# Sums of the second softmax one step later, part of their arithmetic on GpSimd and ScalarE

## Chip, cores and metric

The kernel runs on one core of a Trainium2 chip. The metric is device time of the launch in microseconds, median over runs. An engine here is TensorE (PE in the profile; PEld is its weight load), VectorE (DVE), ScalarE (ACT), GpSimd (POOL) or SyncE (SP, which issues DMAs only).

## The reference

x is 8 x 512 x 32 x 32 in fp32, that is 8 images of 512 channels and 1024 positions. Two attention layers follow each other, each with a residual. Layer 0 is a group norm and a plain attention of 8 heads. The change lies in layer 1:

```python
q, k, v = (einsum('oc,bct->bot', w, gn(x)).reshape(b, 8, 64, t) for w in (w_q, w_k, w_v))
attn = einsum('bhdq,bhdT->bhqT', q, k) * scale        # 8 heads, 1024 x 1024
attn = einsum('gh,bhqT->bgqT', w_head, attn)          # heads are mixed before the softmax
attn = softmax(attn, axis=-1)
mean, var = attn.mean((-2, -1)), attn.var((-2, -1))   # of each image and head
attn = (attn - mean) / sqrt(var + eps) * in_gamma + in_beta
out = einsum('bhqT,bhdT->bhqd', attn, v)              # then a projection and the residual
```

The variance needs, for each row of the softmax, the sum of exp and the sum of exp squared: z and z2 below.

## The kernel before, in words

Layer 1 takes the images one by one (class `Attention1`). The 1024 query positions of an image are cut into NT = 8 blocks. A loop runs rounds p = 0 to 8, each with four steps t = 0 to 3 (`step`). A round is a pipeline of three blocks: it computes the scores of block p, mixes and exponentiates block p-1, and multiplies block p-2 with the values. The whole program is in an order written by hand: each engine executes its instructions in the order of the calls in the source. Between engines, waits follow from the tiles that they share.

The calls within a round, with their engines and the lines of the profile:

- `scores(p, i)`, i = 0 to 7: PE multiplies into a PSUM tile of tag "m" (L1628); ScalarE copies it into `raw` (L1640). In round 0 every second copy is DVE's (L1638).
- `regroup`: SP's DMAs bring `raw` into another layout, `re`.
- `mix(p-1, s)`, s = t: PE mixes the heads (L1665) into two tiles of tag "m"; ScalarE writes the exponentials into `e` (L1678), two instructions. Its matmuls alternate between the two tiles.
- `flip(p-1, s)`: DVE transposes `e` into `et` (L1693). `moments(p-1, s)`: four BN_STATS on DVE give count, mean and squared deviations of `e` (L1704).
- `values(p-2, u, parts)`: PE multiplies `et` with v (L1720) into a PSUM tile of tag "a"; `leave(p-2, u)`: ScalarE copies it out (L1736), two instructions.
- `sums(p-2)`: three instructions on DVE (L1746, L1749, L1750) turn the moments into `zz`, the operand for the sums over partitions.
- `totals(p-2)`: two matmuls (four records in the profile, L1757) with `zz` as weights give z and z2, side by side in one PSUM tile of tag "a". Then `reciprocals`: DVE computes rz = 1/z (L1769); POOL issues two DMAs, rz to DRAM (`zd`, L1772) and back, broadcast, into `rzb` (L1779); DVE keeps z in `zs` (L1782), squares rz (L1784), multiplies by z2 and adds up in `s2` (L1786 to L1789).
- `divide`: in even rounds from 4 on, GpSimd multiplies finished values by `rzb` (L1811).

PSUM has three tiles of tag "m" and two of tag "a"; an allocation waits until the readers of the tile that stood in its place are done. An `Agenda` (`ag.run(slot)`) puts work of the next image at given places: products of v (`v_pair`, L1454; one half is copied out by ScalarE, L1458, the other by DVE, L1459), loads, normalization, and in round 8 the next image's k projection (`k_go`, `k_leave`, and `right_y`, additions on DVE).

After round 8 come `sums` and `totals` of the last block, `instance` (DVE sums `s2` into `isb`) and `instance_end` (the matmul `pi`, L1825, and the image's variance).

Of the kernel before, what the change touches and what calls it, by code (L numbers as in the profile page):

```python
# [9 lines left out]
F32 = mybir.dt.float32  # L10
# [8 lines left out]
P = 128  # L19
# [448 lines left out]
def tile_two_attention_layers(  # L468
# [19 lines left out]
    nc = tc.nc  # L488
# [208 lines left out]
    with ExitStack() as l0:  # L697
# [5 lines left out]
        stat = l0.enter_context(tc.tile_pool(name="stat", bufs=2))  # L703
# [368 lines left out]
        def attention0(b, agenda):  # L1072
# [96 lines left out]
            for i in range(0, NI + 2, 2):  # L1169
                if i < NI:  # L1170
                    scores(i)
                    scores(i + 1)
                if i >= 2:
                    for w in (i - 2, i - 1):
                        values(w)
                        sums(w)
                    if (i - 1) % NG == NG - 1:
                        g = (i - 1) // NG
                        agenda.at(i + 2, lambda g=g: totals(g))
                        agenda.at(i + 6, lambda g=g: reciprocals(g))  # L1180
                        agenda.at(i + 10, lambda g=g: finish(g))
                agenda.run(i)
                agenda.run(i + 1)
# [83 lines left out]
    with ExitStack() as l1:  # L1267
# [6 lines left out]
        stat = l1.enter_context(tc.tile_pool(name="stat1", bufs=2))  # L1274
# [166 lines left out]
        def k_leave():  # L1441
            for fn in due:
                fn()
            due.clear()
# [168 lines left out]
        class Attention1:  # L1613
# [127 lines left out]
            def sums(self, p):  # L1741

                bn = self.bn.pop(p).rearrange("p s a (r k) -> p r (s a) k", k=3)
                zz = stat.tile([P, 3, 2, 16], F32, tag="zz", name=f"zz_{self.b}_{p}")
                mean, m2 = bn[..., 1], bn[..., 2]
                nc.vector.tensor_scalar_mul(  # L1746
                    zz[:, 0::2], mean.unsqueeze(1).to_broadcast([P, 2, 2, 16]), float(2 * P)
                )
                nc.vector.tensor_mul(zz[:, 1], mean, zz[:, 0])  # L1749
                nc.vector.tensor_add(zz[:, 1], zz[:, 1], m2)  # L1750
                self.zz = zz

            def totals(self, p):
# [10 lines left out]
            def reciprocals(self, p, ps):  # L1764

                b = self.b
                z, z2 = ps[:32, 0:32], ps[:32, 32:64]
                rz = stat.tile([32, 32], F32, tag="rz", name=f"rz1_{b}_{p}")
                nc.vector.reciprocal(rz, z)  # L1769
                zd = dram.tile([H, P], F32, tag=f"zd_{b}_{p}", name=f"zd_{b}_{p}")  # L1770
                queue = nc.sync if p == NT - 1 else nc.gpsimd
                queue.dma_start(  # L1772
                    out=zd.rearrange("g (x q) -> x g q", q=4),
                    in_=rz.rearrange("x (g q) -> x g q", q=4),
                )
                if p % 2 == 0:
                    self.rzb = zpool.tile([P, T], F32, tag="rzb", name=f"rzb_{b}_{p}")
                h = p % 2 * D
                queue.dma_start(  # L1779
                    out=self.rzb[h : h + D], in_=zd.rearrange("g i -> (g i)").partition_broadcast(D)  # L1780
                )
                nc.vector.tensor_copy(self.zs[:, p], z)  # L1782
                r2 = stat.tile([32, 32], F32, tag="r2", name=f"r2_{b}_{p}")
                nc.vector.tensor_mul(r2, rz, rz)  # L1784
                if p == 0:
                    nc.vector.tensor_mul(self.s2, r2, z2)  # L1786
                else:
                    nc.vector.tensor_mul(r2, r2, z2)
                    nc.vector.tensor_add(self.s2, self.s2, r2)  # L1789

            def check(self):

# [54 lines left out]
            def step(self, p, t, ag):  # L1847

                new, old, older = p < NT, p >= 1, p >= 2
                if t == 0:  # L1850
                    if new:
                        for i in range(3):
                            self.scores(p, i)
                    if older:
                        self.values(p - 2, 0, 2, 3)
                        self.leave(p - 2, 0)
                        self.sums(p - 2)
                        if p % 2 == 0 and p >= 4:
                            self.divide(p // 2 - 2, nc.gpsimd)
                    if old:  # L1860
                        self.mix(p - 1, 0)
                    ag.run(4 * p - 0.5)
                elif t == 1:
                    if older:
                        self.values(p - 2, 1, 0)
                        self.flip(p - 1, 0)
                        self.totals(p - 2)
                        self.moments(p - 1, 0)
                    if new:
                        self.scores(p, 3)  # L1870
                    if old:
                        self.mix(p - 1, 1)
                    ag.run(4 * p + 0.5)
                elif t == 2:
                    if older:
                        self.values(p - 2, 1, 1)
                    if new:
                        self.scores(p, 4)
                        self.scores(p, 5)
                    if old and not new:  # L1880
                        self.mix(p - 1, 2)
                    ag.run(4 * p + 1.5)
                    if older:
                        self.values(p - 2, 1, 2, 3)
                        self.leave(p - 2, 1)
                    if old and new:
                        self.mix(p - 1, 2)
                else:
                    if new:
                        self.scores(p, 6)  # L1890
                        if old:
                            self.values(p - 1, 0, 0)
                        self.scores(p, 7)
                        if old:
                            self.mix(p - 1, 3)
                            self.values(p - 1, 0, 1)
                    else:
                        self.mix(p - 1, 3)
                        self.values(p - 1, 0, 0, 1)
                    ag.run(4 * p + 2.5)  # L1900
                k_leave()
                if p == 1 or old and t:
                    self.flip(p - 1, t)
                    self.moments(p - 1, t)
                if new:
                    for kh, s in (
                        (), ((0, 0), (0, 1), (0, 2)), ((0, 3),), ((1, 0), (1, 1), (1, 2), (1, 3)),
                    )[t]:
                        self.regroup(p, kh, s)
                if old and t == 0:  # L1910
                    self.piece()
                ag.run(4 * p + t)
# [156 lines left out]
```

## Time and profile before

| | us |
|---|---|
| median of 3 runs | 4002.35 (4001.08 to 4011.55) |
| profiled execution, its own time | 3999.31 |
| span of its profile | 3997.5 |
| PE busy in the span | 3885.5 |
| DVE, ACT, POOL busy | 2834.6, 1971.3, 128.5 |
| layer 1, with the end | from about 1830 on |

The span is the time from the first to the last instruction of the profiled execution. A row of a group gives line, engine, operation, tiles and shapes, then busy time and mean duration (ns), then the engine's idle time just before these instructions and what ended it ("<-"). A row of waits gives who waited for whom, the total in us, how often, and the longest. A line of the order of time gives start, duration, engine, line, operation and tiles, and in brackets the idle time before it. A window line gives its length, each engine's busy time with its number of instructions, the granted clock of TensorE, the busy share of the DMA engines and their rate in GB/s.

### The profile page before, as it was taken

The page shows a single profiled execution, that of the slowest core. Times are in us where ns is not written, and L with a number is a line of the kernel's source. Part 1 is how long each engine was busy: PE and PEld are TensorE (multiplying, and loading weights), DVE is VectorE, ACT ScalarE, POOL GpSimd, SP SyncE. Part 2 cuts the span into 40 slices and gives each one's busy share as a digit, 9 for nine tenths or more (in the row PEclk, how much of TensorE's full clock was granted, in tenths as well). Part 3 has the DMA queues.
Part 4 walks back from the last instruction along what each step waited for, and adds up shares of the span by engine and source line. Part 5 has one row for each costly group of instructions (what it writes and reads, how often), then busy time and mean ns, then how long its engine had stood idle before and what let it go on. Part 6 is the DMA issues. An engine that isn't in the chain of part 4 may idle for free.

```text
span 3997.5 us, 95841 instructions
## 1 busy us (share of the span) xinstructions
PE 3885.5 (97%) x41932; PEld 1826.1 (46%) x41932; DVE 2834.6 (71%) x4124; ACT 1971.3 (49%) x2431; POOL 128.5 (3%) x150
## 2 busy tenths in 40 slices
PE   8999999999999999999999999999999999999997
PEld 4353535344343535344544535545545445445354
DVE  4748475766657584857958949859769679588597
ACT  1726363544536271615717528437257166175274
POOL 0000000000000000000100000000001000000010
PEclk9999999999999999999999999999999999999999
DMA  3313131111121111217828749658469288397384
GB/s 121 120 48 117 46 120 48 62 59 66 53 83 54 72 68 61 75 66 184 230 92 226 190 120 237 173 137 227 148 164 228 99 210 207 97 232 198 107 219 127
DMA packets 245883, 519.10 MB, mean 130 GB/s; under 512 B 47312, under 2 KB 54480, under 8 KB 238800
## 3 DMA queue, kind: packets, MB, share of 16 engines
q1 hardware_dynamic: 238912, 497.95, 43.2%
q0 software_dynamic: 6544, 14.94, 1.7%
q8 instruction: 331, 5.42, 0.6%
q14 instruction: 96, 0.79, 0.1%
HBM read 197.16 MB, written 46.92 MB: 61 GB/s over the span
## 4 chain that ended last, share of the span: by engine, by line
PE 81%; DVE 13%; ACT 2%; DMA 2%; issue 2%; SPq 0%; DVEq 0%
PE s L1084 11%; PE a L1110 11%; PE a L1720 7%; PE s L1628 7%; DVE bn L1704 6%; PE pk_p L902 6%; PE pq_p L902 5%; PE pv L1454 5%; PE pv_p L902 5%; DVE et L1693 5%; PE pp_p L902 5%; PE pk L1379 4%; PE pq L1379 4%; PE pp L1379 4%; PE m L1665 4%
## 5 line engine op out<-in xcount | busy, mean ns | idle before, releaser
L1693 DVE STREAM_TRANSPOSE et<-e 128x2048 f32<-128x2048 f32 x256 | 587.3, 2294 | 88.7 <-ACT e L1678 86.8
L1720 PEld LDWEIGHTS a<-et,v 128*64 128x64 f32 x16384 | 509.2, 138 | 296.2 <-issue 247.6
L1704 DVE BATCH_NORM_STATS2 bn<-e 128x6 f32<-128x512 f32 x1024 | 634.3, 675 | 0.0
L1089 ACT ACTIVATE e<-s 128x1024 f32<-128x1024 f32 x512 | 497.2, 1026 | 234.5 <-PE s L1084 232.1
L1640 ACT COPY raw<-s 128x1024 f32<-128x1024 f32 x480 | 470.2, 1018 | 226.1 <-PE s L1628 197.5
L1720 PE MATMUL a<-et,v 128*64 128x64 f32 x16384 | 557.0, 225 | 12.1 <-DVE et L1693 11.4
L1678 ACT ACTIVATE e<-m 128x1024 f32<-128x1024 f32 x512 | 496.2, 1021 | 126.5 <-PE m L1665 54.2
L1097 DVE TENSOR_TENSOR zacc<-zacc,e 128x1024 f32<-128x1024 f32 x384 | 468.7, 1221 | 87.2 <-ACT e L1089 64.9
L1628 PE MATMUL s<-k,q 64*64 64x512 f32 x4096 | 516.0, 608 | 6.2 <-DVE q L1493 3.1
L1084 PE MATMUL s<-q,k 64*64 64x512 f32 x4096 | 490.1, 593 | 2.3 <-ACT e L1089 2.3
L1110 PE MATMUL a<-e,v 64*64 64x512 f32 x4096 | 484.1, 589 | 0.0
L1665 PE MATMUL m<-re,wmix 32*32 32x512 f32 x8192 | 315.3, 604 | 19.3 <-DMA re<-raw 17.8
L1110 PEld LDWEIGHTS a<-e,v 64*64 64x64 f32 x4096 | 156.7, 133 | 282.8 <-issue 282.2
L1084 PEld LDWEIGHTS s<-q,k 64*64 64x64 f32 x4096 | 147.9, 133 | 275.2 <-issue 240.7
L1628 PEld LDWEIGHTS s<-k,q 64*64 64x64 f32 x4096 | 127.7, 132 | 220.8 <-issue 78.2
L1454 PE MATMUL pv<-wv,y 128*128 128x512 f32 x480 | 212.1, 597 | 0.0
L1736 ACT COPY q<-a 64x256 f32<-64x256 f32 x256 | 93.7, 366 | 184.7 <-PE a L1720 182.7
L1772 POOL DMA_DIRECT2D zd<-rz x56 | 34.7, 619 | 3449.0 <-DVE r L1784 3449.0
L1454 PEld LDWEIGHTS pv<-wv,y 128*128 128x128 f32 x480 | 89.3, 190 | 116.9 <-issue 110.3
L1665 PEld LDWEIGHTS m<-re,wmix 32*32 32x32 f32 x8192 | 66.7, 103 | 148.9 <-ACT raw L1640 58.6
L1458 ACT COPY v<-pv 128x512 f32<-128x512 f32 x30 | 17.6, 585 | 218.7 <-PE pv L1454 218.7
L1095 DVE TENSOR_TENSOR zacc<-e,e 128x1024 f32<-128x1024 f32 x64 | 78.3, 1223 | 56.1 <-ACT e L1089 56.1
(315 smaller groups left out, 3942.4 us busy)
## 6 DMA issues: line engine op xcount, KB each, us to landing
re<-raw SPq DMA_DIRECT2D x1024, 256.0 KB
left_q<-left_q SPq DMA_DIRECT2D x17, 1792.0 KB
left_p<-left_p SPq DMA_DIRECT2D x17, 1792.0 KB
left_k<-left_k SPq DMA_DIRECT2D x10, 1792.0 KB
x<-in_x_dram SPq DMA_DIRECT2D x32, 512.0 KB
rzb<-zd SPq DMA_DIRECT2D x128, 128.0 KB
x<-x SPq DMA_DIRECT2D x64, 256.0 KB
y<-x SPq DMA_DIRECT2D x32, 512.0 KB
```

The costliest lines, as they stand in the source:

```text
L902: nc.tensor.matmul(out, st, mv, start=start, stop=(k == 1), skip_group_check=True)
L1084: nc.tensor.matmul(ps[c * D : c * D + D, m], k[r, hp, k0 : k0 + D], q[r, hp, ts(f, FB)], start=True, stop=True,)
L1089: nc.scalar.activation(e[i], ps, AF.Exp, scale=S0 * S0)
L1110: nc.tensor.matmul(acc[g][a][m * D : m * D + D], v[rows, kc, ts(2 * hp + m, D)], e[i][rows, m], start=(kc == 0), stop=(kc == NG - 1),)
L1379: nc.tensor.matmul(self.ps[m][:, i], w[:, left, k * HC + i * P : k * HC + i * P + P], right[:, k], start=(k == 0 and m != 2), stop=(k == 1 ...
L1454: nc.tensor.matmul(ps[:, m], y_t[b][:, c, ts(2 * i + m, P)], w[:, c], start=(c == 0), stop=(c == NCC - 1),)
L1628: nc.tensor.matmul(ps[c * D : c * D + D, m], qo_t[b][r, p, hp, ts(c, D)], k_t[b][r, hp, ts(kh, FB)], start=True, stop=True,)
L1665: nc.tensor.matmul(ps[a // 2][c * 32 : c * 32 + 32, a % 2].rearrange("p (r h k) -> p h r k", r=2, h=2), wmix[rows].rearrange("p g i -> p ( ...
L1678: nc.scalar.activation(e[:, :, 2 * h : 2 * h + 2].rearrange("p r a k -> p a r k"), ps[h].rearrange("p a (r k) -> p a r k", r=2), AF.Exp,)
L1693: nc.vector.transpose(self.et[p, u].rearrange("p kb (r st a) g q -> p st kb r (a g q)", r=2, st=2)[:, st], self.e[p, s].rearrange("p r a ( ...
L1704: nc.vector.bn_stats(self.bn[p][:, s, a], e[:, :, a].rearrange("p r k -> p k r"))
L1720: nc.tensor.matmul(acc[two * D : two * D + D, s].rearrange("p (x q) -> p x q", q=4), v_t[b][:, kb, ts(g, D)], et[:, kb, :, g], start=(kb = ...
```

## The change

It moves `totals(p-2)` from step 1 of a round to step 2, behind one more piece of `values`. It gives the three instructions of `sums` to GpSimd, with one buffer for `zz` instead of two. In `reciprocals` the copy of z goes from DVE to ScalarE, a new ScalarE copy brings z2 to SBUF (`zq`), and the square, product and addition go to GpSimd, which reads `zq` in place of PSUM. DVE keeps the reciprocal. In round 1 the first flip and its moments are called in step 1 and not at the end of step 0.

```diff
@@ sums
-                zz = stat.tile([P, 3, 2, 16], F32, tag="zz", name=f"zz_{self.b}_{p}")
+                zz = stat.tile([P, 3, 2, 16], F32, tag="zz", name=f"zz_{self.b}_{p}", bufs=1)
                 mean, m2 = bn[..., 1], bn[..., 2]
-                nc.vector.tensor_scalar_mul(
+                nc.gpsimd.tensor_scalar_mul(
                     zz[:, 0::2], mean.unsqueeze(1).to_broadcast([P, 2, 2, 16]), float(2 * P)
                 )
-                nc.vector.tensor_mul(zz[:, 1], mean, zz[:, 0])
-                nc.vector.tensor_add(zz[:, 1], zz[:, 1], m2)
+                nc.gpsimd.tensor_mul(zz[:, 1], mean, zz[:, 0])
+                nc.gpsimd.tensor_add(zz[:, 1], zz[:, 1], m2)
@@ reciprocals
-                nc.vector.tensor_copy(self.zs[:, p], z)
+                nc.scalar.copy(self.zs[:, p], z)
+                zq = stat.tile([32, 32], F32, tag="zq", name=f"zq_{b}_{p}")
+                nc.scalar.copy(zq, z2)
                 r2 = stat.tile([32, 32], F32, tag="r2", name=f"r2_{b}_{p}")
-                nc.vector.tensor_mul(r2, rz, rz)
+                nc.gpsimd.tensor_mul(r2, rz, rz)
                 if p == 0:
-                    nc.vector.tensor_mul(self.s2, r2, z2)
+                    nc.gpsimd.tensor_mul(self.s2, r2, zq)
                 else:
-                    nc.vector.tensor_mul(r2, r2, z2)
-                    nc.vector.tensor_add(self.s2, self.s2, r2)
+                    nc.gpsimd.tensor_mul(r2, r2, zq)
+                    nc.gpsimd.tensor_add(self.s2, self.s2, r2)
@@ step, t == 1
                     if older:
                         self.values(p - 2, 1, 0)
+                    if old:
                         self.flip(p - 1, 0)
-                        self.totals(p - 2)
                         self.moments(p - 1, 0)
@@ step, t == 2
                     if older:
                         self.values(p - 2, 1, 1)
+                        self.totals(p - 2)
@@ step, end of each t
                 k_leave()
-                if p == 1 or old and t:
+                if old and t:
                     self.flip(p - 1, t)
                     self.moments(p - 1, t)
```

## The prediction

> **What bounds the kernel now.** I read the busy line first, then the busy time of one round of layer 1, then the waits of layer 1 (1850 us to the end), then the order of time of one round.
>
> ```profile
> PE 3885.5 (97%) x41932; PEld 1826.1 (46%) x41932; DVE 2834.6 (71%) x4124; ACT 1971.3 (49%) x2431; POOL 128.5 (3%) x150
> ```
> ```profile
> 2149.00:2170.00 21.00, 20.81 (x456) 11.21 (x452) 19.78 (x29) 16.91 (x20) 1.43 (x3) 1.00 0.90 240
> ```
> ```profile
> PE z L1757 <- DVE zz L1750: 29.1, 27, 2.1
> PE m L1665 <- DMA re<-raw: 17.8, 11, 3.3
> PE a L1720 <- DVE et L1693: 10.8, 9, 5.3
> PE z L1757 <- ACT e L1678: 3.6, 18, 0.4
> ```
>
> The first line gives TensorE 97% of the span. The second (columns PE, PEld, DVE, ACT, POOL) is the round p = 3 of image 1: PE is busy 20.81 of 21 us, DVE 19.78, ACT 16.91. So a round is TensorE's, with DVE just behind, and microseconds in which PE stands still are lost for good. The waits say where it stands: 29.1 us before the matmuls of `totals`, for the operand `zz`, and 3.6 more where another semaphore was named but `zz` ended just before; the row of these matmuls has 32.8 us of idle time. That is all that the change can give back there.
>
> [...] The trace shows such an ordering, in the one place where both engines read one PSUM tile (`v_pair`; ScalarE takes the first half, DVE the second):
>
> ```profile
> 2097.28 0.58 ACT L1458 COPY v<-pv 128x512 f32<-128x512 f32 x1 [6.89 <-PE pv L1454]
> ...
> 2097.90 0.69 DVE L1459 COPY v<-pv 128x512 f32<-128x512 f32 x1 [6.44 <-ACT v L1458]
> ...
> 2099.19 1.22 DVE L1638 COPY raw<-s 128x1024 f32<-128x1024 f32 x1 [0.60 <-PE s L1628]
> ...
> 2100.05 1.01 ACT L1640 COPY raw<-s 128x1024 f32<-128x1024 f32 x1 [0.70 <-PE s L1628]
> ```
>
> DVE had been idle for 6.44 us, the matmuls were done, and yet it began only as ScalarE's copy ended. The same two engines, writing one SBUF tile from two PSUM tiles, do overlap (last two lines). So it is the shared PSUM tile that orders them. [...]
>
> **The change part by part.** The key is where `totals` lands. In round 3 of image 1, DVE alone and then ScalarE alone, in order of time:
>
> ```profile
> 2155.54 2.31 DVE L1693 STREAM_TRANSPOSE et<-e 128x2048 f32<-128x2048 f32 x1 [1.05 <-ACT e L1678]
> 2157.78 0.31 DVE L1769 RECIPROCAL rz<-z 32x32 f32<-32x32 f32 x1
> ...
> 2158.65 2.51 DVE L1704 BATCH_NORM_STATS2 bn<-e 128x6 f32<-128x512 f32 x4
> 2161.09 2.28 DVE L1693 STREAM_TRANSPOSE et<-e 128x2048 f32<-128x2048 f32 x1
> ```
> ```profile
> 2153.57 1.94 ACT L1678 ACTIVATE e<-m 128x1024 f32<-128x1024 f32 x2 [0.48 <-ACT q L1736]
> 2156.11 1.01 ACT L1640 COPY raw<-s 128x1024 f32<-128x1024 f32 x1 [0.60 <-PE s L1628]
> 2157.32 1.94 ACT L1678 ACTIVATE e<-m 128x1024 f32<-128x1024 f32 x2 [0.20 <-PE m L1665]
> 2159.30 1.93 ACT L1640 COPY raw<-s 128x1024 f32<-128x1024 f32 x2
> 2162.15 0.74 ACT L1736 COPY q<-a 64x256 f32<-64x256 f32 x2 [0.93 <-PE a L1720]
> ```
>
> The reader is to see that DVE does the reciprocal (L1769) between a flip and its moments, and that ScalarE goes straight from the exponentials of mix 1 (end 2159.26) to the `raw` copies of scores 4 and 5. In the same stretch PE has mix 1 at 2155.97, values, scores 4 and 5, values, and mix 2 at 2162.04.
>
> *Moved to t = 2.* PE's `totals` matmuls now stand behind `values(p-2, 1, 1)`; the reciprocal is queued on DVE behind two whole pairs of flip and moments instead of one flip. The `zz` wait goes: -32.8 us.
>
> *New wait.* The copies `zs` and `zq` read the bank that the reciprocal reads, come after it in the program, and are now ScalarE's; so ScalarE waits for DVE's reciprocal. Queued behind them on ScalarE: the `raw` copies of scores 4 and 5, the leave of the values, the exponentials of mix 2. Who waits: mix 2 on PE, which needs two of the three buffers of tag "m", and one is scores 4's.
>
> Replayed on the round above:
> - DVE can't flip e(p-1, 0) before its exponentials end, at 2155.51. A pair takes 4.61 (2161.09 to the next flip at 2165.70), so two end at 2164.76, and the reciprocal (0.31), which stood at 2157.78, at 2165.07. ScalarE is through with mix 1 at 2158.8.
> - `zs` and `zq`: ACT copies of 256 and 512 columns take 366 and 585 ns, by the slope some 0.17 us for 32: 2165.45. Scores 4's `raw` copy then ends at 2166.46, not 2160.3.
> - PE does values, totals, scores 4 and 5 and half of values and is at mix 2 at 2161.85; it begins at 2166.5: **4.65 us idle**. Its matmuls alternate between both buffers, so the free one does not help.
> - After it `raw` 5, leave (0.74) and the exponentials of mix 2 end at 2170.1 and `raw` 6 at 2171.1; PE is at mix 3 at 2170.7: another 0.45.
> - From there each step of PE, ACT and DVE lies later by the same amount up to the next mix 0, so it comes back each round: 5.1 us.
>
> Rounds 2 to 7 of 8 images: 48 x 5.1 = +245 us. Ends: copies of 0.1 or 0.3 us, a wake-up of 0.1 and the position of DVE's other work give 4.2 to 5.8, or +200 to +280.
>
> *Round 8* has no scores; the reciprocal stands behind two more DVE additions of the next image's `right_y`, at about 1999.8 in image 0 instead of 1990.4. Exponentials 2 end at 2002.15, mix 3 begins then and not at 2000.36: 1.8 us, x8 = +14 (0 to 25).
>
> *Taken from DVE:* per round 219 + 216 + 212 (sums), 116 (`zs`), 179 + 175 + 179 (squares): 1.3 us. PE bounds the round, so beyond the `zz` wait it is worth nothing.
>
> *Put on GpSimd:* six small instructions. [...] The three of the operand are ready some 1 us after moments(p-2, 3), which end near the end of mix 0; `totals` comes 4 us later. Cover: these 4 us, and as much again, since PE waits later anyway. If each took over 1.4 us, the `zz` wait would be back, but inside that stall. The squares stand on POOL's queue behind both DMAs (zd lands 4.1 us after issue) and end over 5 us before the next operand is due. POOL's DMAs and `divide` move with the reciprocal, 7 us later; rzb lands in 6.0, before the next even round. Nothing: 0, at most +10.
>
> *`zz` in one buffer:* the next `sums` wants it a round after the matmuls that read it: 0. *Round 1's flip* one step later: DVE has no instruction between the two places: 0. *Ends of images:* `isb` waits for three GpSimd instructions, about 0.6 us of DVE; PE's `pi` comes at 2023.53, 6 us after the sum was ready: 0, at most +5.
>
> **Sum:** -32.8 + 245 + 14 = +226 on the profiled execution's 3999.31 us (span 3997.5): **4225 us**. The median of the runs is 4002.35, 3 us above that execution; I don't add this.
>
> **The rivals.**
> 1. *No order between the readers.* Then ScalarE gains two copies of 0.2 us in a round in which it has 4 us free, DVE is relieved, and PE loses the 32.8 us: 3999.3 - 33 = 3966, or up to 3985 if transfers, 0.90 to 0.95 busy in rounds 1 to 4, give some back. This ends faster. It decides if ScalarE is past `zs` and `zq` by 2160.8, since `raw` 4 is then ready when PE reaches mix 2; a reciprocal one pair earlier would do as well. Against it: the `v` pair, ordered 23 of 23 times that DVE was idle, and the order of the calls. 9%.
> 2. *A smaller stall.* DVE's pairs, or what stands between the reciprocal and mix 2, are shorter than in this round, or PE's idle time absorbs later waits: 3.7 us a round gives 3999.3 - 33 + 178 + 14 = 4158. The pair has 4.61 to 4.63 us in each of three looked at. 6%.
> 3. *GpSimd late on top*: its operand behind `divide` (2.36 us) and the rzb waits, late by more than 8 us in even rounds. 24 rounds x 4 us more: about 4320. The operand stands ahead of `divide` in its queue. 4%.
>
> **How the numbers follow.** My case: 81%, 4225 with its own 4175 to 4275. The range takes in rival 2 and ends short of rivals 1 and 3: 4150 to 4280. Differences within 0.3% (12 us), about what a measurement of this kernel can tell from no change, get 1%, same 0.01: faster 0.08 (rival 1 but for the case that transfers take its gain back), slower 0.91.
>
> **What would show it.** Right: a row of ScalarE copies `zs<-z` with some 6 us idle each, ended by DVE's reciprocal, about 300 us in all; PE's row `m<-re,wmix` idle by over 200 us, ended by the `raw` copies; rounds of 25.9 us; no wait at L1757's matmuls; DVE idle more, not less. Wrong: `zs` starting before the reciprocal, or rounds of 21 us. If GpSimd's three instructions take over 1.4 us each, the waits at `zz` will show that.

## The result, and the profile after

| | before | after |
|---|---|---|
| median, 4 runs of each on one chip | 4002.43 us (4001.08 to 4011.55) | 4264.14 us (4256.06 to 4266.12) |
| ratio after / before, 95% interval | | 1.0645 [1.0624, 1.0666] |
| profiled execution, its own time | 3999.31 | 4264.97 |
| span | 3997.5 | 4263.1 |
| mean granted TensorE clock | 0.995 | 0.971 |

The change makes the kernel 6.4% slower; on the profiled executions it costs 265.7 us where the sum in the prediction has 226. From one image of layer 1 to the next, 311.81 us pass (277.96 before). Inside an image, the time from one round's sums over partitions to the next's is 27.31 us in the mean of rounds 2 to 7 (21.48 before): 5.83 us more, and five such intervals make 29.2 of the 33.85 us.

First the page of the kernel after: its span and busy line, then four groups, with busy time, mean duration (ns), the idle time just before them, and what ended it.

```profile
span 4263.1 us, 96029 instructions
...
PE 4013.6 (94%) x41932; PEld 1861.4 (44%) x41932; DVE 2760.7 (65%) x3684; ACT 1984.7 (47%) x2559; POOL 251.1 (6%) x526
...
L1693 DVE STREAM_TRANSPOSE et<-e 128x2048 f32<-128x2048 f32 x256 | 590.0, 2305 | 430.7 <-ACT e L1678 425.8
...
L1665 PE MATMUL m<-re,wmix 32*32 32x512 f32 x8192 | 393.3, 638 | 198.4 <-ACT raw L1640 174.3
...
L1746 POOL TENSOR_SCALAR zz<-bn 128x64 f32<-128x64 f32 x64 | 36.0, 563 | 3287.6 <-DVE bn L1704 2869.4
...
L1782 ACT COPY zs<-z 32x32 f32<-32x32 f32 x64 | 11.2, 174 | 335.5 <-DVE rz L1769 335.3
```

The last line is the new row that the prediction asked for: ScalarE stands still for 335.3 us before 64 tiny copies, and DVE's reciprocal ends all of it. The mixing row, L1665, now has 198.4 us of idle time (19.3 before), 174.3 of it ended by ScalarE's `raw` copies. There is no row of L1757 with a wait any more. DVE, relieved of 440 instructions, is less busy (2760.7 against 2834.6) and idles more. And one thing is not explained by waits: PE executes the same 41932 instructions, yet is busy 128 us longer (4013.6 against 3885.5). That is taken up below.

The waits of layer 1 say the same by pairs (total us, times, longest), here PE's and then ScalarE's:

```profile
PE m L1665 <- ACT raw L1640: 174.3, 49, 3.9
PE m L1665 <- DMA re<-raw: 18.5, 14, 3.0
PE a L1720 <- DVE et L1693: 6.1, 8, 1.7
```
```profile
ACT zs L1782 <- DVE rz L1769: 335.3, 56, 7.2
```

One round in order of time, DVE alone:

```profile
2168.07 2.31 DVE L1693 STREAM_TRANSPOSE et<-e 128x2048 f32<-128x2048 f32 x1 [0.76 <-ACT e L1678]
2170.31 2.47 DVE L1704 BATCH_NORM_STATS2 bn<-e 128x6 f32<-128x512 f32 x4
2172.70 2.29 DVE L1693 STREAM_TRANSPOSE et<-e 128x2048 f32<-128x2048 f32 x1
2174.92 2.45 DVE L1704 BATCH_NORM_STATS2 bn<-e 128x6 f32<-128x512 f32 x4
2177.29 0.33 DVE L1769 RECIPROCAL rz<-z 32x32 f32<-32x32 f32 x1
2182.57 2.31 DVE L1693 STREAM_TRANSPOSE et<-e 128x2048 f32<-128x2048 f32 x1 [4.96 <-ACT e L1678]
```

ScalarE and then PE in the same stretch:

```profile
2169.58 1.94 ACT L1678 ACTIVATE e<-m 128x1024 f32<-128x1024 f32 x2 [0.50 <-PE m L1665]
2177.65 0.17 ACT L1782 COPY zs<-z 32x32 f32<-32x32 f32 x1 [6.13 <-DVE rz L1769]
2177.73 0.17 ACT L1784 COPY zq<-z 32x32 f32<-32x32 f32 x1
2177.97 1.93 ACT L1640 COPY raw<-s 128x1024 f32<-128x1024 f32 x2
```
```profile
2174.56 1.05 PE L1665 MATMUL m<-re,wmix 32*32 32x512 f32 x4
2179.03 1.49 PE L1665 MATMUL m<-re,wmix 32*32 32x512 f32 x28 [3.42 <-ACT raw L1640]
2180.45 1.98 PE L1628 MATMUL s<-k,q 64*64 64x512 f32 x8
2182.37 1.47 PE L1720 MATMUL a<-et,v 128*64 128x64 f32 x32
```

DVE does two pairs of transpose and BN_STATS without a gap; the reciprocal stands behind them and ends at 2177.62. ScalarE, through with the exponentials of mix 1 at 2171.52, waits 6.13 us for it, and only then copies scores 4 and 5 to `raw`. PE has begun mix 2 with the four records that fit the free buffer and stands for 3.42 us. Then DVE in its turn has nothing to transpose for 4.96 us. The stall runs once around the three engines.

### The profile page after: what moved, and what is told of

The parts are those of the page before. It is cut to its first block, busy times and chain, and to the rows that moved or that the text cites. A ratio compares the mean times of both kernels' runs of the same rounds, so it can differ in the third digit from the quotient of the medians.

```text
span 4263.1 us, 96029 instructions
## 1 busy us (share of the span) xinstructions
PE 4013.6 (94%) x41932; PEld 1861.4 (44%) x41932; DVE 2760.7 (65%) x3684; ACT 1984.7 (47%) x2559; POOL 251.1 (6%) x526
## 5 line engine op out<-in xcount | busy, mean ns | idle before, releaser
L1693 DVE STREAM_TRANSPOSE et<-e 128x2048 f32<-128x2048 f32 x256 | 590.0, 2305 | 430.7 <-ACT e L1678 425.8
L1720 PEld LDWEIGHTS a<-et,v 128*64 128x64 f32 x16384 | 532.5, 144 | 327.7 <-issue 310.7
L1720 PE MATMUL a<-et,v 128*64 128x64 f32 x16384 | 580.1, 230 | 6.7 <-DVE et L1693 6.7
L1665 PE MATMUL m<-re,wmix 32*32 32x512 f32 x8192 | 393.3, 638 | 198.4 <-ACT raw L1640 174.3
L1628 PE MATMUL s<-k,q 64*64 64x512 f32 x4096 | 554.7, 648 | 6.2 <-DVE q L1493 3.1
L1665 PEld LDWEIGHTS m<-re,wmix 32*32 32x32 f32 x8192 | 80.1, 105 | 372.4 <-ACT raw L1640 238.7
L1628 PEld LDWEIGHTS s<-k,q 64*64 64x64 f32 x4096 | 131.2, 138 | 239.1 <-issue 88.9
L1746 POOL TENSOR_SCALAR zz<-bn 128x64 f32<-128x64 f32 x64 | 36.0, 563 | 3287.6 <-DVE bn L1704 2869.4
L1782 ACT COPY zs<-z 32x32 f32<-32x32 f32 x64 | 11.2, 174 | 335.5 <-DVE rz L1769 335.3
L1736 ACT COPY q<-a 64x256 f32<-64x256 f32 x256 | 93.8, 367 | 135.7 <-PE a L1720 133.6
```

What stands on the lines that cost most here:

```text
L1628: nc.tensor.matmul(ps[c * D : c * D + D, m], qo_t[b][r, p, hp, ts(c, D)], k_t[b][r, hp, ts(kh, FB)], start=True, stop=True,)
L1665: nc.tensor.matmul(ps[a // 2][c * 32 : c * 32 + 32, a % 2].rearrange("p (r h k) -> p h r k", r=2, h=2), wmix[rows].rearrange("p g i -> p ( ...
L1693: nc.vector.transpose(self.et[p, u].rearrange("p kb (r st a) g q -> p st kb r (a g q)", r=2, st=2)[:, st], self.e[p, s].rearrange("p r a ( ...
L1720: nc.tensor.matmul(acc[two * D : two * D + D, s].rearrange("p (x q) -> p x q", q=4), v_t[b][:, kb, ts(g, D)], et[:, kb, :, g], start=(kb = ...
```

## The experiments

All ratios are to the kernel before, run on the same chip, with 95% intervals.

**1. The order of the calls on ScalarE.** From the kernel after, the two copies are put ahead of the reciprocal, so that DVE waits for ScalarE and not the other way round:

```diff
+                nc.scalar.copy(self.zs[:, p], z)
+                zq = stat.tile([32, 32], F32, tag="zq", name=f"zq_{b}_{p}")
+                nc.scalar.copy(zq, z2)
                 nc.vector.reciprocal(rz, z)
...
-                nc.scalar.copy(self.zs[:, p], z)
-                zq = stat.tile([32, 32], F32, tag="zq", name=f"zq_{b}_{p}")
-                nc.scalar.copy(zq, z2)
```

> The changed kernel with the two ScalarE copies of z and z2 placed ahead of the reciprocal, nothing else. Theory A (ScalarE's queue stands behind DVE's reciprocal because the readers of one PSUM tile take turns in the order of the program): ScalarE then waits for PE only, DVE waits for ScalarE's copies that are long done; the stall before mix 2 goes, and with it the halved clock after it; PE also keeps the 32.8 us of waits at zz that the change saved: 3966 us, up to 3985 if the transfers give some back. Theory B (what costs is the added work on ScalarE and GpSimd, or the later place of totals): all that is still there, so about 4264, at least over 4200. Idle before zs: under 0.5 us each under A, some 6 us under B.

Measured: 4059.86 us, ratio 1.0134 [1.0116, 1.0151], a round of 22.75 us. Three lines in another place give back 204 of the 262 us. ScalarE's wait for the reciprocal is gone: before `zs` it now stands still for 2.3 us in all, and for PE's sums. But it is not a gain: 56 us above the kernel before, some 75 to 95 above what the theory had.

**2. The copies back on DVE**, all else as in the kernel after:

```diff
-                nc.scalar.copy(self.zs[:, p], z)
+                nc.vector.tensor_copy(self.zs[:, p], z)
-                nc.scalar.copy(zq, z2)
+                nc.vector.tensor_copy(zq, z2)
```

> The changed kernel with the copies zs and zq given to DVE, so that all readers of z are on one engine; the place of totals and the GpSimd work stay. Theory A: no engine waits for another's read, 3966 to 3985 us, as close to e1_scalar_first as 0.3%; the 0.23 us that DVE does more per round lie in its slack. Theory B with GpSimd or the place as the cause: 4200 or more. B with ScalarE's added work as the cause: also near 3970, but then e1_scalar_first stays at 4264.

Measured: 4062.7 us, ratio 1.0140 [1.0123, 1.0157], a round of 22.89 us: the same as with ScalarE first, and the same unexplained rest.

**3. ScalarE's copies alone, at the old place.** From the kernel before: `zs` and `zq` by ScalarE behind the reciprocal, DVE keeps the arithmetic (and reads `zq`), `zz` has one buffer, `totals` stays in step 1. The copies in the diff:

```diff
-                nc.vector.tensor_copy(self.zs[:, p], z)
+                nc.scalar.copy(self.zs[:, p], z)
+                zq = stat.tile([32, 32], F32, tag="zq", name=f"zq_{b}_{p}")
+                nc.scalar.copy(zq, z2)
```

> The kernel before with only the two copies on ScalarE (after the reciprocal), squares on DVE from zq, zz in one buffer; totals stays in step 1, where the reciprocal has one flip ahead of it and not two pairs of flip and moments. Theory A: the stall has the length by which the reciprocal lies behind the point where ScalarE is free. Here that is 2.4 us and not 6.3; replayed on round 3 of image 1, PE is held up at scores 4 and 5 by 1.4 us a round, with no halved clock: 48 x 1.4 = 67, less what the waits at zz had taken anyway: 4040 to 4070 us. Theory B (GpSimd or step 2 costs): 4002, unchanged.

Measured: 4066.65 us, ratio 1.0151 [1.0134, 1.0168], a round of 22.56 us, as expected. One wait of PE's and one of ScalarE's:

```profile
PE s L1628 <- ACT raw L1640: 50.8, 40, 1.5
```
```profile
ACT zs L1782 <- DVE rz L1769: 133.6, 56, 2.6
```

At the old place the reciprocal has only a transpose ahead of it on DVE, not two whole pairs, and ScalarE's wait per round is 2.4 us (133.6 / 56) in place of 6.0 (335.3 / 56). PE meets it at the scores, which need the tiles that `raw` empties. So the copies cost 62 us without the move; the move makes the same wait two and a half times as long.

**4. The move alone.** From the kernel before, `totals` in step 2, everything else DVE's as it was:

```diff
                         self.values(p - 2, 1, 0)
                     self.flip(p - 1, 0)
-                        self.totals(p - 2)
...
                         self.values(p - 2, 1, 1)
+                        self.totals(p - 2)
```

> The kernel before with totals moved from step 1 to step 2 and nothing else: all readers of z and all arithmetic stay on DVE. Theory A: the place itself costs nothing and the waits at zz go, 32.8 us: about 3970 us (3965 to 3985). Theory B, that the later place costs through the later reciprocal, rzb and divide: 4200 or more.

Measured: 4077.94 us, ratio 1.0177 [1.0160, 1.0194], a round of 23.10 us. Both theories missed. The waits of PE show why:

```profile
PE a L1720 <- DVE r L1788: 51.4, 38, 3.0
PE m L1665 <- DMA re<-raw: 48.2, 32, 4.3
PE a L1720 <- DVE s L1786: 12.8, 8, 1.6
```

In one round, DVE's last reader of z, and PE around it:

```profile
2178.45 0.17 DVE L1788 TENSOR_TENSOR r<-r,z 32x32 f32<-32x32 f32 x1
```
```profile
2176.38 1.10 PE L1628 MATMUL s<-k,q 64*64 64x512 f32 x8
2178.68 1.15 PE L1720 MATMUL a<-et,v 128*64 128x64 f32 x32 [1.20 <-DVE r L1788]
```

The first values of a new block, `values(p-1, 0, 0)`, need a PSUM tile of tag "a". There are two. With `totals` in step 2, the one handed to them is z's, and they start only when the last instruction that reads z has ended. In the kernel before no such wait is in the list. DVE comes to it late, behind its two pairs; 64.2 us of PE's time go there, and the wait for the regrouped scores (`re<-raw`) grows from 17.8 to 48.2 us besides. With ScalarE first the same wait is there under another name, since DVE's only read of z is then the reciprocal (L1772 in that kernel); in experiment 2 it is 49.7 us:

```profile
PE m L1665 <- DMA re<-raw: 46.7, 31, 4.6
PE a L1720 <- DVE rz L1772: 43.1, 45, 2.6
```

Together these come near the 56 us of experiment 1, as an estimate: 43.1, and 28.9 more for the transfers, and 16.5 more inside the mixing groups (38.5 us beyond 1.15 us a group, 22.0 in the kernel before), less the 32.8 of `zz`.

**5. The operand alone on GpSimd**, the place and everything else as before:

```diff
-                nc.vector.tensor_scalar_mul(
+                nc.gpsimd.tensor_scalar_mul(
...
-                nc.vector.tensor_mul(zz[:, 1], mean, zz[:, 0])
-                nc.vector.tensor_add(zz[:, 1], zz[:, 1], m2)
+                nc.gpsimd.tensor_mul(zz[:, 1], mean, zz[:, 0])
+                nc.gpsimd.tensor_add(zz[:, 1], zz[:, 1], m2)
```

> The kernel before with the three instructions of the sums' operand on GpSimd and nothing else, totals in step 1. GpSimd needs 1.1 to 1.2 us for them where DVE needed 0.72, so zz comes 0.5 us later after the moments, while DVE is free 0.65 us a round earlier. Where PE waits for zz it waits about 0.5 us longer: up to 4020 us; where DVE's backlog caused the wait, part comes back: 4000 at least.

Measured: 4013.18 us, ratio 1.0030 [1.0018, 1.0041], as expected. The wait before `totals` is longer than DVE's was (29.1 and 3.6):

```profile
PE z L1757 <- POOL zz L1750: 46.2, 47, 2.1
```

So GpSimd is the slower engine for these three, by little (1.18 us together in the kernel after, 0.65 on DVE in the kernel before); one step later that is covered, as the next experiment shows: it has no wait for `zz`.

**6. z's tile freed early.** The first experiment once more, and the reciprocal now reads ScalarE's copy, so that DVE does not touch that PSUM tile at all:

```diff
-                nc.vector.reciprocal(rz, z)
+                nc.vector.reciprocal(rz, self.zs[:, p])
```

> As e1_scalar_first, with DVE's reciprocal taken from the SBUF copy zs and not from PSUM, so that ScalarE is the only reader of z and DVE does not touch that PSUM tile. Theory C (found in e1, e2 and e4: the next values take the PSUM tile of z, and wait there for DVE's last read of it, some 1 us a round): the wait of PE at the first values of step 3 goes, the waits at zz stay away, 3966 to 3985 us. Rival D (what e1 lost lies in the transfers, whose waits had grown to 47 us): they stay, 4020 to 4060.

Measured: 4004.51 us, ratio 1.0004 [0.9995, 1.0013], a round of 21.70 us: between what the two theories had. PE's waits:

```profile
PE m L1665 <- DMA re<-raw: 29.1, 22, 3.9
PE a L1720 <- DVE et L1693: 9.3, 8, 4.9
```

The wait for z's tile is gone, as is that for `zz`; yet the time is that of the kernel before, not 33 us less. The transfers' wait is 11 us longer, and more of it lies inside the mixing groups, where the trace has it as stretched groups and not as idle time ahead of them: what these groups take beyond their usual 1.15 us comes to 47.6 us in layer 1, and to 22.0 in the kernel before. The same with operand and squares back on DVE (and round 1's flip where it was):

> As e7_scalar_first_rz_from_sbuf, with the sums' operand and the squares back on DVE: the kernel before with totals in step 2, ScalarE's two copies first, and the reciprocal and squares from SBUF. Theory C says that no wait hangs on GpSimd: within 0.5% of e7, 3970 to 3995 us, the 1.2 us that DVE does more per round being near its slack. If GpSimd's part is what keeps DVE from falling behind, this one shows waits at et or zz again and is slower than e7 by 10 us or more.

Measured: 4008.1 us, ratio 1.0011 [1.0003, 1.0019]: as near to the other as expected, and like it above what the theory had. GpSimd's part is worth 0.1% of the time at most; the two intervals overlap.

**7. Do the transfers take the gain?** Half of the DMAs of `regroup` in blocks 2 to 7 are left out (`mix` then reads old data there), once in the kernel of experiment 6, once, as a control, in the kernel before:

```diff
-                for r in range(2):
+                for r in range(2 if p < 2 else 1):
```

> As e7_scalar_first_rz_from_sbuf, but of the regrouping DMAs of blocks 2 to 7 only the first of each two is issued, so half of these rows stay as an earlier block left them; transfers of a round fall from 16 of 256 KB to 8. Theory G (what e7 did not gain went to the transfers: raw tiles and re slots are waited for): the waits for re<-raw (29 us) and the waits inside the mix groups (some 25 us more than before) go; rounds of 20.8 us; 3945 to 3970 us. Theory H (they are waits of another kind, or latency that traffic does not set): 3990 to 4005.

> The kernel before with the same half of the regrouping DMAs left out in blocks 2 to 7: the control for e9. Waits for re<-raw (17.8 us) go, in part, and the waits at zz (32.8 us) stay: 3980 to 3995 us under theory G. The difference e10 minus e9 is then what the change of e7 is worth when transfers do not limit: about 30 us; under theory H it is about 0.

Measured: 3944.51 us, ratio 0.9856 [0.9831, 0.9881], and 3971.75 us, ratio 0.9925 [0.9899, 0.9950]. The first lies at the lower end of what its theory had, the control some 8 us below what was expected of it. First the waits of the kernel of experiment 6 with fewer DMAs, then those of the kernel before with fewer:

```profile
PE a L1720 <- DVE et L1693: 10.0, 8, 5.5
PE m L1665 <- DMA re<-raw: 6.3, 8, 2.0
```
```profile
PE z L1757 <- DVE zz L1750: 23.8, 25, 2.1
PE a L1720 <- DVE et L1693: 10.7, 9, 5.3
PE z L1757 <- ACT e L1678: 5.5, 24, 1.1
PE m L1665 <- DMA re<-raw: 3.8, 7, 1.3
```

With fewer transfers the two kernels stand 27 us apart, about the 29.3 us that the second still waits for `zz`; with all transfers they stand level. So 27 of the 33 us can be had, and in the full kernel the regrouping DMAs take them back. Of the 25.6 us more inside the mixing groups, 10 stay with fewer DMAs (29.4 us against 19.3); their cause is not shown.

**8. The clock after the stall.** In the kernel after, matmuls were put into the stall of mix 2, to see whether its cost is the idle time alone. Twice they went into `mix`, for s = 2, ahead of its own matmuls, into the first or the (p % 2)-th of its two tiles:

```diff
+                if s == 2 and 1 <= p < NT - 1:
+                    for _ in range(4):
...
+                                nc.tensor.matmul(
+                                    ps[0][c * D : c * D + D, m], qo_t[b][r, p, 0, ts(c, D)],
+                                    k_t[b][r, 0, ts(0, FB)], start=True, stop=True,
+                                )
```

> The changed kernel with four more groups of score products ahead of mix 2 in rounds 2 to 7, written into the tile that mix 2 then overwrites: added work of about 3.8 us, in place of idle time of about 4.3. Theory E (the part of the loss above the replay is TensorE's granted clock, halved for 3.4 us after each stall): the products after the stall run at full rate again, a round takes about 26 us in place of 27.3, and the time falls although work is added: about 4220 us (4205 to 4240). Rival F (the products after the stall are slow for another reason): no gain, 4264 or above.

> As e5_filled_stall, with the added products written in each round into that one of mix 2's two tiles that is free early (in e5 every other round took the one that waits for raw 4, so its products came after the stall; these rounds took 32 us, the others 25.7). Theory E: all rounds take about 25.75 us in place of 27.3, 48 x 1.55 = 74 us less than the changed kernel although work is added: 4190 us (4180 to 4215). Rival F (no clock effect): 4264 or above.

Measured: 4347.36 us, ratio 1.0862 [1.0846, 1.0878], and 4346.39 us, ratio 1.0862 [1.0834, 1.0889]. Both missed. Rounds alternate between 25.7 and some 32 us: in one the added products stand in the stall, in the next they wait for a tile that comes free only after it, and the stall follows on top. The second was to pick the free tile by the block's parity and did not; which tile is free early was not settled. Even so the two say something of the clock: in both, the 24 rounds with the filled stall (25.4 us in the mean) have no period of halved clock, and each of the 24 long ones has one. A third form needs no tile of its own, as scores 5 are computed five times over into their own tile, ahead of the stall:

```diff
-                for c in range(2):
+                for c in [0, 1] * (5 if i == 5 and p >= 2 else 1):
```

> The changed kernel with the products of scores 5 issued five times over into the same tile in rounds 2 to 7 (the last writes the result): 3.7 us of added products in each round, in a tile that is free when PE comes to it in every round, ahead of the values and of mix 2, and so inside the stall. Theory E (the loss above the replay is the clock halved after each stall): no round has a halved clock after mix 2, each takes about 25.8 us in place of 27.3: about 4190 us (4180 to 4215), less than the changed kernel with 180 us of products added. Rival F: 4264 or above.

Measured: 4193.85 us, ratio 1.0489 [1.0469, 1.0508], a round of 25.69 us. PE does more work, and the kernel is 70 us faster than without it (62 by the two ratios). The page's busy line, one round (columns: PE, PEld, DVE, ACT, POOL, granted clock, DMA share, GB/s), and PE's waits:

```profile
PE 4105.1 (98%) x43468; PEld 1897.2 (45%) x43468; DVE 2755.0 (66%) x3684; ACT 1981.1 (47%) x2559; POOL 251.2 (6%) x526
```
```profile
2170.00:2196.00 26.00, 25.74 (x501) 12.77 (x487) 18.87 (x21) 17.30 (x24) 2.67 (x8) 1.00 0.77 195
```
```profile
PE m L1665 <- DMA re<-raw: 15.8, 10, 3.0
PE m L1665 <- ACT raw L1640: 11.4, 48, 0.5
```

The added products fill the stall: the wait for `raw` falls from 174.3 to 11.4 us. The round stays near the 25.9 us of the replay, as ScalarE's wait for the reciprocal is still there (339.4 us). What disappears is the time beyond that. The windows of the kernel after show what that was: the stall itself, the 3.40 us that follow, the rest up to the next mix, and the whole round.

```profile
2176.00:2179.00 3.00, 0.00 (x0) 0.00 (x0) 1.62 (x4) 1.29 (x4) 0.69 (x1) 1.00 0.30 74
2179.70:2183.10 3.40, 3.40 (x42) 1.04 (x24) 0.53 (x1) 3.32 (x6) 1.03 (x3) 0.50 0.41 93
2183.10:2190.00 6.90, 6.90 (x130) 3.20 (x128) 6.08 (x6) 5.25 (x7) 0.00 (x0) 1.00 0.75 175
2170.40:2197.10 26.70, 23.28 (x459) 11.75 (x455) 18.75 (x21) 17.06 (x23) 2.68 (x7) 0.94 0.78 187
```

After the stall the granted clock is 0.50 for 3.40 us. The group of eight score matmuls takes 1.98 us in it (2180.45 in PE's order of time above) and 1.09 to 1.10 elsewhere, that of 32 value matmuls 1.47 and not 1.15. At a share of 0.50, 3.40 us cost up to 1.7, by an estimate; the round is 27.31 where the replay gives 25.9. Of the 128 us by which PE is busier, the half-begun mixing groups (1.05 us for four records) account for some 44, by an estimate (48 x 0.9); the rest is put down to the halved clock. Over layer 1 the records have 50 such periods with 249.1 us together, against 6 with 35.5 in the kernel before and 2 with 14.6 with scores 5 repeated. The length counts too: of the 48 rounds with a stall, 27 have 3.41 us at half the clock and take 26.8 us in the mean from mix 0 to mix 0, and 21 have 6.83 us and take 27.6.

## Why the prediction was right, point by point

*"The `zz` wait goes": held.* No wait at L1757 is left, nor is there one in experiment 6, which has no stall: one step later the operand is ready in time. Its price of 32.8 us is that of the wait, and experiments 6 and 7 show that it becomes time only where the transfers leave room.

*"So ScalarE waits for DVE's reciprocal": held, and it is most of the loss.* The row of `zs` shows 335.3 us where about 300 were forecast, 6.0 us each; taking the order away (experiments 1 and 2) takes 201 to 204 us away. The copy takes 0.174 us and starts 0.03 us after the reciprocal's end (2177.62 and 2177.65 in the round above), where the prediction allowed up to 0.3 and 0.1. What the prediction leaned on shows an order by tile and no more: in the `v` pair ScalarE and DVE read different halves of one PSUM tile, 512 columns each, and all 23 times that DVE stood idle before its half (128.3 us) it was ScalarE's copy that ended the wait. What asks for this order was not shown. The stall before mix 2 was to be 4.65 us. The trace has 3.42 us of idle time before the 28 remaining records, and the four that had gone ahead into the free buffer are listed as busy for 1.05 us, where an eighth of such a group (1.14 us whole, elsewhere) takes 0.14: with the 0.9 us over that, 4.3 us in all. This split is also why the mixing row shows 174.3 us of waits and not over 200.

*The round of 25.9 us: the mechanism was right, the size was off.* It is 27.31. The step that failed is "From there each step of PE, ACT and DVE lies later by the same amount": it takes the durations after the stall from a round without one. PE's were up to 1.8 times as long, at half the clock. The term of 5.1 us a round was 5.1 + 1.4; the round with the stall filled by other products, 25.69 us, shows the replay's value without that. 48 x 1.4 = 67 us; the total was off by 265.7 - 226 = 40 only, since other terms went the other way. So the number was in part lucky: with the 0.7 us that the `zz` wait had taken, a round pays 27.31 - 21.48 + 0.7 = 6.5 us, outside the 4.2 to 5.8 that the prediction gave as its ends.

*Round 8, +1.8 us an image: not seen.* Counted from mix 0 to mix 0, rounds 2 to 7 take 27.17 us each in the mean (21.46 before), and six times these 5.71 us make 34.3 us more an image. From mix 0 of round 8 to the first mix of the next image it is 128.76 us (129.21 before): 0.45 us less, not 1.8 more. In images 0 to 6 mix 3 of round 8 begins 6.72 us after mix 2 in both kernels. Over 8 images that is some 18 us less than the prediction has.

*"The three of the operand are ready some 1 us after moments(p-2, 3)", the author's estimate: mostly held.* These three GpSimd instructions take 1.18 us together, 0.563 for the first (128x64 elements), 0.346 and 0.268 for the others (128x32); those of the squares take 0.241 to 0.248. Before `isb` DVE waits 1.2 us an image for them (9.4 us, 8 times), where the prediction had some 0.6. Their cover held: no wait of PE's names any of the six in the kernel after, and with everything on DVE (second part of experiment 6) the time differs by 0.1%. Nor do they slow DVE's long instructions by much: a transpose takes 2305 ns (2294 before), a BN_STATS 679 (675).

*What the prediction left out.* The list of waits that the move adds has no word of z's PSUM tile, which at the new place goes to the next block's first values. In the kernel after it costs little: by the time PE has been through the stall, z has been read, and no wait names its tile. Where there is no stall (experiments 1, 2 and 4) it came to light, with 43 to 64 us of PE's time and a longer wait for the transfers. So rival 1's 3966 us lacked a term: without an order between the readers the change would hardly have been faster; experiments 1 and 2, where ScalarE waits for no read of DVE's, are 1.3 and 1.4% slower. That rival and the next two did not come about. Rival 2's smaller stall, 3.7 us a round, is excluded by the round; rival 3 would show waits at `zz`, and there are none.

*What stays open.* Why the transfers take the 33 us back in experiment 6 is shown only as far as experiment 7 goes: fewer DMAs, and most of the gain is there. ScalarE's `raw` copies wait there for the DMAs that read the same tile 4 times, 3.3 us in all (20 times and 17.8 us in the kernel before); what these waits cost the round was not tested by itself. How much of the extra transfer wait in experiments 1 and 4 belongs to the same cause was not measured either.

## What to carry to other kernels

Before a small copy moves to another engine, look for who else reads the same PSUM tile: here the later reader in the program waited for the earlier one (335.3 us in 56 waits), and with it everything that is queued behind it; put the engine whose queue has the urgent work first, or let the second read an SBUF copy. A tile that moves in time also changes who inherits its buffer, so ask of each new place which allocation comes next and what its last reader is queued behind. And when a stall of some microseconds comes back each round, look whether TensorE works on at half the clock after it, as it did here (0.50 for 3.41 or 6.83 us after each of 48 stalls), and add that to its idle time.

## What the runs showed of the hardware that was not expected

A stall like the one shown, 4.3 us with 3.4 of them listed as idle, was enough here for TensorE's clock to be halved: the records have it in each of the 48 rounds (2 to 7 of 8 images). Of the 50 periods with a granted clock of 0.50 in layer 1, 28 last 3.41 us, 21 just twice that, 6.83, and the last, at the end of the program, 10.22; the trace has no share but 1.00 and 0.50. All 50 begin a whole number of times 3.413 us apart: 700 times that make the 2389.3 us from the first (1865.7 us) to the last (4255.0). PE did not have to stand still for as long as a period lasts: in the 27 rounds with one period of 3.41 us, PE's records leave it idle for 2.2 to 3.3 of the 3.41 us just ahead of it, and busy for the rest (the ends of matmuls are modelled). What sets the start and the length of a period was not shown.

What this makes of a stall could be seen only by filling it: 163 us of products added to the kernel after (row L1628: 678.6 us busy with them, 516.0 in the kernel before) made it 70 us faster. Where a group of matmuls begins in a free buffer and ends in one that is awaited, its records carry no idle time for the first part (four records, 1.05 us); the wait is then smaller in the list than on the clock.
